# Pinning VectorE's reads of layer 0's fourth and fifth products between the sums of the output projection's left factors

## Chip, core and metric

The kernel runs on one core of a Trainium2 chip. The metric is the device time of one execution in microseconds (us), taken as the median of several runs. Five engines work side by side on the core. TensorE (PE in the profile, with its weight loads in a row of their own, PEld) does the matmuls and writes them to PSUM, the accumulation memory. VectorE (DVE) and ScalarE (ACT) read PSUM and work on SBUF, the on-chip memory. GpSimd (POOL) works on SBUF, and SyncE (SP) issues the transfers. Each engine runs its own instructions in the order in which the compiled program holds them, and waits on semaphores for the others.

## What is computed

64 graphs of 256 nodes with 512 features pass two layers that share one adjacency matrix. The reference, cut to what matters here:

```python
# layer 0: graph convolution, residual, layer norm
mi, mj = x @ Wi.T, x @ Wj.T
h = layernorm(x + deg[:, None] * (mi + b) + a @ mj)
# layer 1: masked attention of 8 heads of width 64, residual, layer norm
q, k, v = split_heads(h @ Wq.T + bq), ...(Wk, bk), ...(Wv, bv)
attn = softmax(where(adj == 0, -inf, q @ k.T / 8))
out = layernorm(h + merge_heads(attn @ v) @ Wo.T + bo)
```

Everything is float32.

## The kernel before

The 64 graphs are worked through in 32 groups of two. While the attention of one group runs, layer 0 of the next group runs between its steps. All large products use a seven-product scheme in place of the eight block products of a 2 x 2 block matrix multiplication. The left factors are the four blocks `A11`, `A12`, `A22` (and `A21`) and four sums of them, `S1` to `S4`. A product is eight matmuls (x 256 columns) and adds up in one PSUM bank. VectorE adds the bank to a tile in SBUF when a product is done; two of the banks are then accumulated into once more:

```python
def combine_left(f, order=anywhere):                       # L469
    nc.vector.tensor_add(f["S1"], f["A21"], f["A22"])      # L470
    nc.vector.tensor_sub(f["S2"], f["S1"], f["A11"])       # L471
    order(nc.vector.tensor_sub(f["S3"], f["A11"], f["A21"]))   # L472
    nc.vector.tensor_sub(f["S4"], f["A12"], f["S2"])       # L473

def l0_steps(b):                                           # layer 0, one graph
    ...
    def add_to(dst, src):
        nc.vector.tensor_add(dst, src, dst)                # L530
    ...
    def step4():
        product("y", "S2", T2, True)                       # fourth product
        add_to(place(0, 1), banks["y"])
    def step5():
        product("z", "S1", T1, True)                       # fifth product
        add_to(place(1, 1), banks["z"])
    def step6():
        product("y", "S3", T3, False)                      # adds to what is in bank y
        add_to(h, banks["y"]...)                           # both halves of a row block
        norm(xh[b][:, 1, :])
    def step7():
        product("z", "S4", B22, False)                     # adds to what is in bank z
        add_to(place(0, 1), banks["z"])
        norm(xh[b][:, 0, :])
```

So the seventh product may start only when VectorE has read what the fifth left in bank `z`, and the sixth only when it has read bank `y`.

`in_order` and `anywhere` say how the compile-time scheduler may place an instruction. `in_order` pins it behind the instruction that was written just before it for the same engine; `anywhere` leaves the scheduler free to place it by its own estimate of when it is ready. All matmuls are pinned, so TensorE follows the program text.

The place that the change is about comes once in each of the 31 turns of the main loop, after the last two pairs of heads of a group. `o` holds the steps of the output projection of group g (`o[0]` and `o[1]` use blocks of the attention's output that need no sums, later ones use `S1` to `S4` of `oS`, which `combine_left` makes). `rest` holds steps 4 to 7 of layer 0 for the second graph of group g + 1:

```python
inverses = divide_at_once(g, w + 1)   # twice: a reciprocal (L814), then a multiply into aoT (L815)
o = o_steps(g)
rest = work[SLOTS]
run(o[:1] + rest[:1] + o[1:2] + rest[1:2])
combine_left(oS[g], in_order)
end_values(inverses)                  # GpSimd: rtot += rden, twice (L820)
run(rest[2:] + o[2:5] + work[SLOTS + 1] + o[5:6] + work[SLOTS + 2] + o[6:])
```

`o[0]` ends in a ScalarE copy of its bank and two GpSimd additions to `xh` (L697 and L698, the second over 128 x 1024 elements). `o[1]` ends in a VectorE addition of its bank to `xh` (L691). The tile names in the profile are these: `po` is a bank of layer 0, `st` a bank of the projections, `xS` holds the left sums of layer 0, `oS` those of the output projection, and `aoT` is the attention's output. Every matmul has line L281, that of a helper.

Of the kernel before, what the change touches and what calls it, by code (L numbers as in the profile page):

```python
# [225 lines left out]
def unshifted_path(ctx, tc, flag, x, adj, wiT, wjT, b0, wqT, bq, wkT, bk, wvT, bv, woT, bo, out):  # L226
# [13 lines left out]
    nc = tc.nc  # L240
# [25 lines left out]
    def bank(name):  # L266
        return ps_m.tile([P, 512], F32, tag="mm", name=name)

    def score_banks(name):
        return ps_s.tile([P, 2, 512], F32, tag="sc", name=name)  # L270
# [9 lines left out]
    def matmul(*args, **kw):  # L280
        in_order(nc.tensor.matmul(*args, **kw))  # L281

    def transpose(*args):
        in_order(nc.tensor.transpose(*args))
# [6 lines left out]
    def load_x(b):  # L291
        if b < B:
            xh[b] = p6.tile([P, NT, D], F32, tag="xh", name="xh")
            nc.sync.dma_start(out=xh[b], in_=x[b].rearrange("(t p) d -> p t d", p=P))
# [67 lines left out]
    xhi, xlo, xl, xS, hT, hS, qT, kT, vv, aoT, oS = ({} for _ in range(11))  # L362
# [99 lines left out]
    def norm(t):  # L462
        norm_apply(t, *norm_stats(t))
# [2 lines left out]
        return {"A11": a11, "A12": a12, "A21": a21, "A22": a22,  # L466
                "S1": s[:, 0], "S2": s[:, 1], "S3": s[:, 2], "S4": s[:, 3]}

    def combine_left(f, order=anywhere):  # L469
        nc.vector.tensor_add(f["S1"], f["A21"], f["A22"])  # L470
        nc.vector.tensor_sub(f["S2"], f["S1"], f["A11"])  # L471
        order(nc.vector.tensor_sub(f["S3"], f["A11"], f["A21"]))  # L472
        nc.vector.tensor_sub(f["S4"], f["A12"], f["S2"])  # L473


    def input_tiles(b):
# [39 lines left out]
    def l0_steps(b):  # L516
        banks = {}

        def product(name, lname, n, first):
            if first:  # L520
                banks[name] = bank("po")[:, :H]
            for c in range(NC):
                matmul(banks[name], xS[b][lname][:, c, :], w0[:, n, c, :], start=(first and c == 0),
                                 stop=(c == NC - 1), skip_group_check=True)

        def place(t, j):
            return xh[b][:, t, j * H:(j + 1) * H]

        def add_to(dst, src):
            nc.vector.tensor_add(dst, src, dst)  # L530

        def step1():
            product("x", "A11", B11, True)
            u1 = p2.tile([P, H], F32, tag="lu", name="u1")
            nc.scalar.copy(u1, banks["x"])

            rest = xh[b].rearrange("p t (j o) -> p (t j) o", j=2)[:, 1:]
            nc.gpsimd.tensor_tensor(rest, rest, u1.unsqueeze(1).to_broadcast([P, 3, H]), ALU.add)  # L538

        def step2():  # L540
            product("w", "A22", T4, True)
            add_to(place(1, 0), banks["w"])

        def step3():
            product("x", "A12", B21, False)
            add_to(place(0, 0), banks["x"])

        def step4():
            product("y", "S2", T2, True)
            add_to(place(0, 1), banks["y"])  # L550

        def step5():
            product("z", "S1", T1, True)
            add_to(place(1, 1), banks["z"])

        def step6():
            product("y", "S3", T3, False)
            h = xh[b][:, 1, :].rearrange("p (j o) -> p j o", j=2)
            add_to(h, banks["y"].unsqueeze(1).to_broadcast([P, 2, H]))
            norm(xh[b][:, 1, :])  # L560

        def step7():
            product("z", "S4", B22, False)
            add_to(place(0, 1), banks["z"])
            norm(xh[b][:, 0, :])

        return [step1, step2, step3, step4, step5, step6, step7]

    def h_transpose(b, t, borrow=False):

        g, i = divmod(b, NB)
        if i == 0 and t == 1:
            hT[g] = p1.tile([P, NC, NB * N], F32, tag="hT", name="hT")
            hS[g] = pair_blocks(hT[g], "hS")
        pt = (score_banks("pt_h")[:, 0, :] if borrow else bank("pt_h")).rearrange("p (c n) -> p c n", c=NC)
        for c in range(NC):
            transpose(pt[:, c, :], xh[b][:, t, c * P:(c + 1) * P], ident)
        nc.scalar.copy(hT[g][:, :, i * N + t * P:i * N + (t + 1) * P], pt)
        if t == 0 and i == NB - 1:
            combine_left(hS[g])  # L580

    def add_output_bias(b):

# [3 lines left out]
    def pair_blocks(m, tag):  # L587

        s = p1.tile([P, 4, 2, N], F32, tag=tag, name=tag)
        return left_blocks(m[:, 0:2, 0:N], m[:, 2:4, 0:N], m[:, 0:2, N:2 * N], m[:, 2:4, N:2 * N], s)  # L590
# [186 lines left out]
    def values(g, w):  # L777
        i, pr = divmod(w, NC)
        if w == 0:
            aoT[g] = p1.tile([P, NC, NB * N], F32, tag="aoT", name="aoT")  # L780
            oS[g] = pair_blocks(aoT[g], "oS")
        pp = w % 2
        if pp == 0:
            pavs[g] = ps_v.tile([P, 2, N], F32, tag="av", name="pav")
        pe, _ = made[g, w]
        for kc in range(NT):
            for j in range(2):
                h0 = (2 * pr + j) * DH
                matmul(pavs[g][j * DH:(j + 1) * DH, pp, :], vv[g][:, i, kc, h0:h0 + DH], pe[:, j, kc, :],
                       start=(kc == 0), stop=(kc == NT - 1))  # L790

    def multiply():
        while products:
            d, spread = products.pop()
            in_order(nc.gpsimd.tensor_tensor(d, d, spread, ALU.mult))

    def divide_two(g, w):

        dst = target(g, w)
        nc.scalar.copy(dst, pavs[g])  # L800
        divide(dst, [made.pop((g, w - 1))[1], made.pop((g, w))[1]])

    def divide_at_once(g, w):


        den = bank("den").rearrange("p (r q) -> p r q", r=2)
        for pp in range(2):
            _, pk = made.pop((g, w - 1 + pp))
            for j in range(2):
                matmul(den[j * DH:(j + 1) * DH, pp, :], ones[:, :DH], pk[:, j, :], start=True, stop=True)  # L810
        inverses = []
        for pp in range(2):
            inverses.append(p2.tile([P, N], F32, tag="rden", name="rden"))
            in_order(nc.vector.reciprocal(inverses[pp], den[:, pp, :]))  # L814
            in_order(nc.vector.tensor_mul(target(g, w)[:, pp, :], pavs[g][:, pp, :], inverses[pp]))  # L815
        return inverses
# [29 lines left out]
    def layer0(g):  # L846

        b1, b2 = NB * g, NB * g + 1

        def item(f, *args):  # L850
            return lambda: f(*args)

        p, q = l0_steps(b1), l0_steps(b2)
        return [[item(l0_inputs, b1, 0, True), item(l0_inputs, b1, 1)],
                p[0:3] + [item(split_x, b2)] + p[3:4],
                p[4:7] + [item(l0_inputs, b2, 0)],
                [item(l0_inputs, b2, 1), q[0], q[1], item(h_transpose, b1, 1, True),
                 q[2], item(h_transpose, b1, 0, True)],
                q[3:],
                [item(h_transpose, b2, 1, True)], [item(h_transpose, b2, 0, True)]]  # L860

    def run(steps):
        for s in steps:
            s()
# [54 lines left out]
    for g in range(NG - 1):  # L919
        load_x(NB * (g + 2))  # L920
        load_x(NB * (g + 2) + 1)
        work = layer0(g + 1)
        run(work[0])
        for w in range(2, NB * NC, 2):
            values(g, w - 2)
            values(g, w - 1)
            multiply()
            divide_two(g, w - 1)
            later = [scores(g, w), scores(g, w + 1)]
            part = work[w // 2]  # L930
            n = 0 if w == NB * NC - 2 else 1
            run(later[:n] + part[:1] + later[n:] + part[1:])
        w = NB * NC - 2
        values(g, w)
        values(g, w + 1)
        multiply()
        inverses = divide_at_once(g, w + 1)
        o = o_steps(g)
        rest = work[SLOTS]
        run(o[:1] + rest[:1] + o[1:2] + rest[1:2])  # L940
        combine_left(oS[g], in_order)
        end_values(inverses)
        run(rest[2:] + o[2:5] + work[SLOTS + 1] + o[5:6] + work[SLOTS + 2] + o[6:])
        end = finish_steps(g)
        q = qk_steps(g + 1, qT, "qT", bq_sb, bqd)
        k = with_output_bias(g + 1, qk_steps(g + 1, kT, "kT", bk_sb, bkd))
        v = v_steps(g + 1)
        run(q[:5] + end[:1] + q[5:6] + end[1:2] + q[6:7] + end[2:3] + k[:1] + end[3:4] + k[1:] + end[4:] + v[:1])
        split_x(NB * (g + 2))
        run(v[1:5])  # L950
        run([scores(g + 1, 0), scores(g + 1, 1)])
        run(v[5:])
# [3 lines left out]
    g = NG - 1  # L956
# [89 lines left out]
```

## Time and profile before

| | before |
|---|---|
| median of 3 runs | 3230.88 us (3230.29 to 3233.19) |
| span of the profiled run | 3230.8 us |
| TensorE matmuls busy | 3189.2 us, 99% |
| TensorE weight loads busy | 2617.4 us, 81% |
| VectorE busy | 1892.0 us, 59% |
| GpSimd busy | 1506.9 us, 47% |
| ScalarE busy | 1113.0 us, 34% |
| granted TensorE clock | 0.998 |

The busy times are sums of instruction durations, so a stretch in which two matmuls overlap counts once and a gap not at all. One turn of the main loop takes about 99.7 us: the first and the last of the 31 instructions that make `S1` of `oS` start at 143.4 and 3134.1 us, and (3134.1 - 143.4) / 30 = 99.69.

In a timeline, the columns are the start and the duration in us, the engine, the line, the operation, what it writes and reads, the shape, and how many instructions of one kind were merged. In brackets stands the idle time of the engine before it and the instruction that ended this idle time. In a table of waits, the columns are the engine, tile and line that waited, the one it waited for, the total in us, how often, and the longest.

### The profile page before, as it was taken

The page shows a single profiled execution, that of the slowest core. Times are in us where ns is not written, and L with a number is a line of the kernel's source. Part 1 is how long each engine was busy: PE and PEld are TensorE (multiplying, and loading weights), DVE is VectorE, ACT ScalarE, POOL GpSimd, SP SyncE. Part 2 cuts the span into 40 slices and gives each one's busy share as a digit, 9 for nine tenths or more (in the row PEclk, how much of TensorE's full clock was granted, in tenths as well). Part 3 has the DMA queues.
Part 4 walks back from the last instruction along what each step waited for, and adds up shares of the span by engine and source line. Part 5 has one row for each costly group of instructions (what it writes and reads, how often), then busy time and mean ns, then how long its engine had stood idle before and what let it go on. Part 6 is the DMA issues. An engine that isn't in the chain of part 4 may idle for free. (4 is left out here: it accounts for less than half of the span.)

```text
span 3230.8 us, 48219 instructions
## 1 busy us (share of the span) xinstructions
PE 3189.2 (99%) x17398; PEld 2617.4 (81%) x17398; DVE 1892.0 (59%) x3847; ACT 1113.0 (34%) x2146; POOL 1506.9 (47%) x1191
## 2 busy tenths in 40 slices
PE   8999999999999999999999999999999999999998
PEld 6888888888888888888888888888888888888885
DVE  6655556555565555655556655556555565555665
ACT  2333333333333333333333333333333333333333
POOL 3454444544445444455444454344544445444443
PEclk9999999999999999999999999999999999999999
DMA  7234432344323433223443234432334322444223
GB/s 246 64 107 122 121 97 74 102 118 123 112 66 92 120 121 118 74 87 111 123 123 90 74 106 121 121 106 67 99 119 123 113 69 90 118 121 119 80 70 92
DMA packets 257168, 340.90 MB, mean 106 GB/s; under 512 B 29856, under 2 KB 154272, under 8 KB 256928
## 3 DMA queue, kind: packets, MB, share of 16 engines
q1 hardware_dynamic: 256928, 337.76, 34.9%
q8 instruction: 143, 2.34, 0.3%
q14 instruction: 97, 0.79, 0.1%
HBM read 274.73 MB, written 37.75 MB: 97 GB/s over the span
## 5 line engine op out<-in xcount | busy, mean ns | idle before, releaser
L454 POOL TENSOR_TENSOR rstd<-ve,mhalf 128x1 f32<-128x1 f32 x256 | 140.6, 549 | 813.6 <-DVE below L452 813.0
L281 PE MATMUL po<-w,xS 128*128 128x256 f32 x2048 | 474.9, 382 | 4.4 <-DVE xh L530 0.5
L281 PE MATMUL st<-hS,factor 128*128 128x256 f32 x2048 | 454.4, 380 | 2.5 <-DVE u L636 2.5
L763 POOL TENSOR_TENSOR pk<-pe 128x512 f32<-128x512 f32 x256 | 322.1, 1274 | 276.9 <-ACT pe L760 276.9
L281 PEld LDWEIGHTS po<-w,xS 128*128 128x128 f32 x2048 | 384.4, 190 | 77.4 <-DVE xh L530 17.2
L281 PEld LDWEIGHTS st<-hS,factor 128*128 128x128 f32 x2048 | 390.2, 191 | 56.3 <-DVE u L636 2.9
L281 PE MATMUL po<-w,xl 128*128 128x256 f32 x1536 | 360.1, 384 | 16.8 <-DVE xS L492 15.9
L760 ACT ACTIVATE pe<-pe 128x1024 f32<-128x1024 f32 x256 | 270.2, 1057 | 248.2 <-DVE pe L756 248.2
L281 PEld LDWEIGHTS po<-w,xl 128*128 128x128 f32 x1536 | 284.0, 190 | 73.3 <-PE po L281 22.9
L281 PE MATMUL st<-hT,factor 128*128 128x256 f32 x1536 | 342.2, 379 | 1.0 <-DVE qT L667 1.0
L636 DVE TENSOR_TENSOR u<-st,u 128x512 f32<-128x512 f32 x96 | 66.4, 692 | 468.8 <-PE st L281 461.6
L756 DVE TENSOR_TENSOR pe<-ps,maskT 128x1024 f32<-128x1024 f32 x256 | 297.1, 1201 | 67.6 <-PE ps L281 67.6
L530 DVE TENSOR_TENSOR xh<-po,xh 128x256 f32<-128x256 f32 (+1 forms) x384 | 170.5, 458 | 268.2 <-POOL xh L538 197.1
L281 PEld LDWEIGHTS st<-hT,factor 128*128 128x128 f32 x1536 | 291.7, 190 | 40.9 <-DVE qT L667 1.4
L281 PE MATMUL ps<-qT,kT 64*128 64x256 f32 x2048 | 256.5, 389 | 0.0
L281 PE MATMUL pav<-pe,v_sb 128*64 128x256 f32 x2048 | 250.1, 386 | 1.9 <-ACT pe L760 1.8
L281 PEld LDWEIGHTS ps<-qT,kT 64*128 64x128 f32 x2048 | 187.0, 186 | 68.2 <-issue 51.3
L281 PE MATMUL st<-factor,hS 128*128 128x256 f32 x1024 | 234.8, 382 | 0.0
L281 PE MATMUL st<-factor,oS 128*128 128x256 f32 x992 | 229.4, 379 | 0.0
L833 DVE RECIPROCAL rden<-den 128x256 f32<-128x256 f32 x96 | 168.8, 1758 | 91.6 <-PE den L281 86.1
L281 PEld LDWEIGHTS st<-factor,hS 128*128 128x128 f32 x1024 | 191.9, 190 | 35.4 <-issue 10.6
L459 ACT ACTIVATE shift<-below,rstd 128x1 f32<-128x1 f32 x256 | 75.4, 294 | 415.2 <-POOL rstd L454 409.6
(112 smaller groups left out, 5035.9 us busy)
## 6 DMA issues: line engine op xcount, KB each, us to landing
xh<-in_x_dram SPq DMA_DIRECT2D x64, 512.0 KB, 4.0
factor<-wq SPq DMA_DIRECT2D x128, 256.0 KB, 2.7
factor<-wk SPq DMA_DIRECT2D x128, 256.0 KB, 2.6
factor<-wv SPq DMA_DIRECT2D x128, 256.0 KB, 4.3
factor<-wo SPq DMA_DIRECT2D x124, 256.0 KB, 2.7
out_dram<-xh SPq DMA_DIRECT2D x62, 512.0 KB, 4.1
factor<-in_wqT_dram SPq DMA_DIRECT2D x96, 256.0 KB, 2.7
factor<-in_wkT_dram SPq DMA_DIRECT2D x96, 256.0 KB, 2.7
```

Of the source, the lines that this page charges most:

```text
L281: in_order(nc.tensor.matmul(*args, **kw))
L454: nc.gpsimd.tensor_tensor(rstd, ve, mhalf, ALU.pow)
L459: order(nc.scalar.activation(shift, below, AF.Identity, scale=rstd))
L530: nc.vector.tensor_add(dst, src, dst)
L636: nc.vector.tensor_add(new("u2"), bank["y"], k["u1"])
L756: nc.vector.tensor_add(pe.rearrange("p j t q -> p j (t q)"), ps.rearrange("p j t q -> p j (t q)"), maskT.rearrange("p t q -> p (t q)").uns ...
L760: in_order(nc.scalar.activation(flat, flat, AF.Exp, scale=QSCALE, accum_out=etot[:, NB * g + i, pr:pr + 1]))
L763: nc.gpsimd.tensor_tensor(pk, pe[:, :, 0, :], pe[:, :, 1, :], ALU.add)
L833: nc.vector.reciprocal(rden, den)
```

## The change

The four sums become a list of steps, so that other work can be written between them, and each of them can be pinned. At the end of the last two pairs of heads the first sum is moved ahead of layer 0's fifth product, and the other three follow it. The additions that read layer 0's fourth and fifth products are pinned as well. The aim is a fixed order on VectorE in which the bank of the fifth product is read right behind the first sum.

```diff
-    def combine_left(f, order=anywhere):
-        nc.vector.tensor_add(f["S1"], f["A21"], f["A22"])
-        nc.vector.tensor_sub(f["S2"], f["S1"], f["A11"])
-        order(nc.vector.tensor_sub(f["S3"], f["A11"], f["A21"]))
-        nc.vector.tensor_sub(f["S4"], f["A12"], f["S2"])
+    def left_steps(f, order=anywhere):
+        return [lambda: order(nc.vector.tensor_add(f["S1"], f["A21"], f["A22"])),
+                lambda: order(nc.vector.tensor_sub(f["S2"], f["S1"], f["A11"])),
+                lambda: order(nc.vector.tensor_sub(f["S3"], f["A11"], f["A21"])),
+                lambda: order(nc.vector.tensor_sub(f["S4"], f["A12"], f["S2"]))]
...
-        def add_to(dst, src):
-            nc.vector.tensor_add(dst, src, dst)
+        def add_to(dst, src, order=anywhere):
+            order(nc.vector.tensor_add(dst, src, dst))
...
         def step4():
             product("y", "S2", T2, True)
-            add_to(place(0, 1), banks["y"])
+            add_to(place(0, 1), banks["y"], in_order)
 
         def step5():
             product("z", "S1", T1, True)
-            add_to(place(1, 1), banks["z"])
+            add_to(place(1, 1), banks["z"], in_order)
...
         if t == 0 and i == NB - 1:
-            combine_left(hS[g])
+            for step in left_steps(hS[g]):
+                step()
...
-        run(o[:1] + rest[:1] + o[1:2] + rest[1:2])
-        combine_left(oS[g], in_order)
+        left = left_steps(oS[g], in_order)
+        run(o[:1] + rest[:1] + o[1:2] + left[:1] + rest[1:2] + left[1:])
         end_values(inverses)
```

No instruction is added or removed, and none changes its shape. The pins on steps 4 and 5 hold for all 64 graphs, not at this place alone. The sums of `hS`, the left factors of the query, key and value projections, stay free as they were.

## The prediction, made before the run

> **What bounds the kernel now.** I read the totals first, then the table of waits for TensorE, then the timeline of one turn of the main loop at the place that the diff touches.
>
> The totals give TensorE's matmuls 99% of the span, and no other engine more than 59%:
>
> ```profile
> PE 3189.2 (99%) x17398; PEld 2617.4 (81%) x17398; DVE 1892.0 (59%) x3847; ACT 1113.0 (34%) x2146; POOL 1506.9 (47%) x1191
> ```
>
> A change that only orders VectorE's instructions can therefore win no more than the time in which TensorE stands still: 3230.8 - 3189.2 = 41.6 us, 1.3% of the span. It could lose more than that. The table of waits says whether any of these 41.6 us belongs to the two reads that the diff pins. These are the rows of the weight loads, with total us, times and longest:
>
> ```profile
> PEld po L281 <- PE po L281: 22.9, 31, 1.1
> ...
> PEld po L281 <- DVE xh L530: 17.2, 32, 0.9
> ```
>
> The second row is the one. L530 is layer 0's addition that reads a bank, and `po` is that bank. It makes a weight load wait 32 times for 17.2 us in all; 31 of these are the turns of the main loop, 0.53 us each (31 x 0.53 = 16.4), and one of 0.9 us is in the start-up. The first row, also once a turn, belongs to an earlier product that waits for layer 0's inputs, and the diff doesn't touch it.
>
> The timeline of one turn in the middle of the run shows how the wait comes about:
>
> ```profile
> 1538.05 1.89 PE L281 MATMUL st<-factor,aoT 128*128 128x256 f32 x8
> ...
> 1538.42 2.36 POOL L698 TENSOR_TENSOR xh<-xh,u 128x1024 f32<-128x1024 f32 x1
> 1538.80 0.36 DVE L530 TENSOR_TENSOR xh<-po,xh 128x256 f32<-128x256 f32 x1
> 1539.08 0.41 DVE L815 TENSOR_TENSOR aoT<-pav,rden 128x256 f32<-128x256 f32 x1
> 1539.56 3.43 PEld L281 LDWEIGHTS po<-w,xS 128*128 128x128 f32 x16
> 1539.59 1.73 DVE L470 TENSOR_TENSOR oS<-aoT 128x512 f32<-128x512 f32 x1
> 1539.77 5.73 PE L281 MATMUL po<-w,xS 128*128 128x256 f32 x24
> ...
> 1540.72 1.19 POOL L820 TENSOR_TENSOR rtot<-rtot,rden 128x256 f32<-128x256 f32 x1
> 1541.24 0.68 DVE L691 TENSOR_TENSOR xh<-st,xh 128x512 f32<-128x512 f32 x1
> 1541.84 0.68 DVE L471 TENSOR_TENSOR oS<-oS,aoT 128x512 f32<-128x512 f32 x1
> 1542.44 0.68 DVE L472 TENSOR_TENSOR oS<-aoT 128x512 f32<-128x512 f32 x1
> 1543.04 0.41 DVE L530 TENSOR_TENSOR xh<-po,xh 128x256 f32<-128x256 f32 x1
> 1543.38 0.68 DVE L473 TENSOR_TENSOR oS<-aoT,oS 128x512 f32<-128x512 f32 x1
> 1543.51 1.59 PEld L281 LDWEIGHTS po<-w,xS 128*128 128x128 f32 x8 [0.53 <-DVE xh L530]
> ...
> 1545.34 1.89 PE L281 MATMUL st<-factor,aoT 128*128 128x256 f32 x8
> ```
>
> The 24 matmuls at 1539.77 are three products: layer 0's fifth (bank z), sixth (bank y) and seventh (bank z again). The seventh may not start before VectorE has read the fifth. That read is the L530 at 1543.04. The fifth product was done at about 1539.77 + 1.89 = 1541.66 (1.89 is what eight matmuls take in the first row), but VectorE then first made `S2` (L471) and `S3` (L472). The read ended at 1543.45, and the seventh product's weights went in at 1543.51, 0.53 us after they could have.
>
> What TensorE itself loses is less than 0.53, because the loads run ahead of the matmuls and catch up a little. From 1538.05 to 1539.77 one product takes 1.72 us, start to start. Three take 3 x 1.72 = 5.16; the trace has 1545.34 - 1539.77 = 5.57. **The loss is 0.41 us a turn**, or 12.7 us over 31 turns. A second reckoning: 24 matmuls of another layer 0 graph, at 1512.33 in the same turn, took 5.45 us, and 24 of the value projection at 1579.03 took 5.34, against 5.73 here; that is 0.28 to 0.39. I take 0.41, from the starts, as ends are modelled.
>
> **What the Trainium skill says.** Three places bear on this.
>
> - "TensorE: Matmul & The Clock Gate", Step-by-step: matmuls stay in program order, and only weight loads are pulled ahead. So TensorE can't fill the gap with the output projection's product behind it. The trace agrees: the product that follows starts at 1545.34, after all 24, though its inputs (`aoT`, the multiply L815) were complete at 1539.5 and the bank it writes had been read by 1541.9 (L691).
> - "SBUF — State Buffer", Who interferes with whom: a VectorE instruction with two SBUF inputs contends with a GpSimd instruction that reads SBUF, whoever starts first holds the port, and the other blocks fully; with at most one SBUF input it does not contend. The trace agrees. `S1` of `oS` (L470) takes 1.73 us here and 2.06 on average over 31, while the same sum for `hS` takes 0.68 on average over 32. Here it ends at 1541.32, 0.54 after the GpSimd addition L698 ended at 1540.78. The L691 and L530 additions, with one input in PSUM, keep their usual lengths.
> - "Perfetto Trace Analysis", Identifying the Most-Contended Engine: matmul occupancy is no good measure of headroom in TensorE. I use the 41.6 us only as a ceiling on what waits can cost; the gain itself comes from starts.
>
> **The change part by part.** No work is added or removed. What is written for VectorE in this stretch now is: second multiply (pinned), read of y (pinned), read of x (L691, free), `S1` (pinned), read of z (pinned), `S2`, `S3`, `S4` (pinned). A pin holds an instruction behind the one written before it, so this chain is fixed, except that the read of x might move up; its product ends too late for that. In the times of the turn above:
>
> 1. The second multiply follows the reciprocal directly, about 1538.9 to 1539.3, and the read of y comes behind it, 1539.25 to 1539.65. It was 0.45 earlier before. The sixth product loads its first weights at 1539.56 + 1.72 = 1541.28, so 1.6 us of slack remain.
> 2. The read of x is no longer behind `S1`. Its product ends at 1538.05 + 1.89 = 1539.94, so it runs at about 1540.0 to 1540.7. VectorE stands idle for some 0.4 us ahead of it. That costs nothing, for `S1` would have been blocked in this time.
> 3. `S1` is issued at about 1540.6 and is still held by L698 until 1540.78. It ends where it ended, at about 1541.33. The move of the read of x into the blocked time is what pays for everything after it.
> 4. The read of z waits for its product, 1541.66, and runs from 1541.7 to 1542.1. The weights of the seventh product want to load at 1543.51 - 0.53 = 1542.98. **The wait is gone, with 0.9 us to spare.**
> 5. `S2`, `S3`, `S4` follow at 0.60 us a step, and end at about 1543.9 instead of 1544.06. The first product that needs one of them comes in the load row behind 1545.13 + 1.73 = 1546.86 at the earliest: no new wait. The read of the sixth product follows at about 1543.85 (was 1543.98), and the norms behind it are no later than before. The transposes that need them start at 1550.5 in TensorE's row; the norm's last step for them ended at 1547.59. TensorE is 0.4 earlier now, and over 2 us of slack remain.
>
> Sum on TensorE's path: 31 x -0.41 = -12.7 us. Nothing is added to it. The pins at the other places change nothing that I can see: the trace already has the reads of y and z behind what is written before them (y behind two reads at 1506.43, z at 1514.42 behind the mask additions). Work that TensorE itself triggers moves up with it, so the gain should carry to the end. 3230.9 - 12.7 = 3218.2; I give back 0.3 for small changes in the schedule: **3218.5 us**, 0.4% less.
>
> **Rivals.**
>
> - *GpSimd takes the port first.* If L820 starts ahead of `S1`, `S1` waits another 0.73 us (the length of an unblocked L820), and ends near 1542.05; z is then read from 1542.0 to 1542.4, still 0.5 us in time. Against it: VectorE asks first. Time: the same 3218.
> - *The wait only changes its name.* `S1` written ahead of the read of z could hold it up when L698 runs late. It would have to be late by 0.9 us before TensorE waits again. L698 is triggered by TensorE's own product and in the trace lies within some tenths in every turn that I looked at (first, eighth, fifteenth, sixteenth, twenty-third, last). With half of the gain left: 3224 to 3225.
> - *The gain is given back later.* Some other chain of the turn, set by GpSimd or VectorE, could end last once TensorE is 0.4 earlier. For it: GpSimd and VectorE do run for long stretches without a gap. Against it: both have idle time that waits for TensorE in every turn, so they move with it. Time: 3226 to 3231.
> - *A pin hurts elsewhere.* The scheduler places by its own estimates; a read that it must now hold back, in any of the 64 graphs, could make TensorE wait. A tenth of a microsecond in each graph would cost 6 us. Time: 3225 to 3240.
>
> **Range and chances.** I give the full gain about 80%, and a little more or less of it comes from the two reckonings (0.28 to 0.41 a turn: 8.7 to 12.7 us). The other ways share the rest, mostly with part of the gain. The range is 3214.5 to 3226. A gain of 2% would need 65 us, more than all of TensorE's standing time, and a loss of 2% would need 2.1 us a turn; both are near zero.
>
> **What would show it.** Right: the row of weight loads that wait for L530 falls from 32 times and 17.2 us to about once and under 1 us. The 24 matmuls take about 5.3 us instead of 5.73. VectorE shows the order multiply, y, x, `S1`, z, `S2`, `S3`, `S4`, and `S1` takes about 0.7 to 0.8 instead of 2.06 on average, since it is issued late. A turn takes 99.28 us instead of 99.69. Wrong: a new waiter of TensorE at `po` or `st` with 31 entries, or an unchanged turn although this wait is gone. The prediction would fail if the scheduler moved something that I hold fixed.

## The result, and the profile after

The changed kernel takes 3219.63 us (median of 6 runs, 3216.64 to 3220.97), against 3231.64 us before (6 runs, 3230.29 to 3233.19). The ratio is 0.9961, with a 95% interval of 0.9949 to 0.9974: 12.0 us less. The prediction was 3218.5 us.

The totals of the changed kernel, on its page:

```profile
PE 3179.5 (99%) x17398; PEld 2625.4 (82%) x17398; DVE 1847.1 (57%) x3847; ACT 1108.6 (34%) x2146; POOL 1505.3 (47%) x1191
```

The number of instructions is the same on all engines. VectorE is busy for 44.9 us less than before (1892.0), though it does the same work; the reason is in `S1`, below. TensorE's stretches without work went from 41.6 to 3217.3 - 3179.5 = 37.8 us, 3.8 us less, though the time fell by 12.0. The rest was booked as busy. Each of the 24 matmuls below is recorded with a duration of 0.38 us, but they start 5.18 / 24 = 0.216 us apart. The record of one matmul therefore covers the first 0.16 us of a gap behind it, and the first matmul behind the gap is recorded as 0.48 us long. Of the 0.39 us that a turn lost before, only 0.12 us show as idle; over 31 turns these are the 3.8 us.

The weight loads' rows in the table of waits of the changed kernel:

```profile
PEld po L281 <- PE po L281: 23.2, 31, 1.1
...
PEld po L281 <- DVE xh L530: 0.9, 1, 0.9
```

The second row had 32 waits and 17.2 us. Only that of the start-up is left. The first row is as it was.

A turn of the changed kernel's main loop, in its timeline (the diff adds one line, so the former L691, L698, L815 and L820 are now L692, L699, L816 and L821):

```profile
1531.67 2.37 POOL L699 TENSOR_TENSOR xh<-xh,u 128x1024 f32<-128x1024 f32 x1
1531.82 0.42 DVE L816 TENSOR_TENSOR aoT<-pav,rden 128x256 f32<-128x256 f32 x1
1532.16 0.41 DVE L530 TENSOR_TENSOR xh<-po,xh 128x256 f32<-128x256 f32 x1
1532.81 5.16 PEld L281 LDWEIGHTS po<-w,xS 128*128 128x128 f32 x24
1533.03 5.34 PE L281 MATMUL po<-w,xS 128*128 128x256 f32 x24
...
1533.30 0.69 DVE L692 TENSOR_TENSOR xh<-st,xh 128x512 f32<-128x512 f32 x1 [0.72 <-PE st L281]
1533.90 0.68 DVE L470 TENSOR_TENSOR oS<-aoT 128x512 f32<-128x512 f32 x1
1533.98 1.19 POOL L821 TENSOR_TENSOR rtot<-rtot,rden 128x256 f32<-128x256 f32 x1
1534.95 0.42 DVE L530 TENSOR_TENSOR xh<-po,xh 128x256 f32<-128x256 f32 x1 [0.37 <-PE po L281]
1535.30 0.68 DVE L471 TENSOR_TENSOR oS<-oS,aoT 128x512 f32<-128x512 f32 x1
...
1538.21 1.89 PE L281 MATMUL st<-factor,aoT 128*128 128x256 f32 x8
```

The three products are one unbroken run of 24 matmuls. From their start to that of the next product it is 1538.21 - 1533.03 = 5.18 us, where it was 5.57. VectorE waits 0.37 us for the fifth product and reads it at once, from 1534.95 to 1535.37. `S1` (L470) takes 0.68 us; it had taken 1.73 in the turn shown before, 2.06 on average. A turn takes (3122.8 - 143.6) / 30 = 99.31 us by the starts of `S1`, 0.38 less than before, and 31 x 0.38 = 11.8 us.

### The profile page after: what moved, and what is told of

Same layout as the page of the kernel before. It is cut to its first block, busy times and chain, and to the rows that moved or that the text cites. A ratio compares the mean times of both kernels' runs of the same rounds, so it can differ in the third digit from the quotient of the medians.

```text
span 3217.3 us, 48188 instructions
## 1 busy us (share of the span) xinstructions
PE 3179.5 (99%) x17398; PEld 2625.4 (82%) x17398; DVE 1847.1 (57%) x3847; ACT 1108.6 (34%) x2146; POOL 1505.3 (47%) x1191
## 5 line engine op out<-in xcount | busy, mean ns | idle before, releaser
L281 PE MATMUL po<-w,xS 128*128 128x256 f32 x2048 | 467.2, 382 | 0.5 <-DVE xh L530 0.5
L761 ACT ACTIVATE pe<-pe 128x1024 f32<-128x1024 f32 x256 | 270.3, 1057 | 248.2 <-DVE pe L757 248.2
L281 PEld LDWEIGHTS po<-w,xl 128*128 128x128 f32 x1536 | 284.5, 191 | 72.2 <-PE po L281 23.2
L530 DVE TENSOR_TENSOR xh<-po,xh 128x256 f32<-128x256 f32 (+1 forms) x384 | 172.4, 463 | 279.7 <-POOL xh L538 197.0
L692 DVE TENSOR_TENSOR xh<-st,xh 128x512 f32<-128x512 f32 x186 | 144.9, 779 | 135.0 <-PE st L281 133.9
```

What stands on the lines that cost most here:

```text
L530: order(nc.vector.tensor_add(dst, src, dst))
L761: in_order(nc.scalar.activation(flat, flat, AF.Exp, scale=QSCALE, accum_out=etot[:, NB * g + i, pr:pr + 1]))
```

## The experiments

The change does four things to VectorE's order: the multiply comes ahead of the read of y, the read of x comes ahead of `S1`, the read of z comes ahead of `S2` and `S3`, and `S1` is out of GpSimd's way. My theory was that only one thing counts: the moment at which z is read. If that is later than the moment at which the seventh product's weights could load, TensorE loses time. Without a wait these weights go in 3.45 us after the first weights of the fifth product. The rivals: `S1` no longer held up by GpSimd is the gain; the pins in all 64 graphs are; or the read of x, moved into the blocked time, "is what pays for everything after it", as the prediction put it.

| kernel | VectorE's order | weights wait for z, a turn | time | ratio to before, 95% |
|---|---|---|---|---|
| before | y, mult, `S1`, x, `S2`, `S3`, z, `S4` | 0.53 us | 3231.6 | |
| changed | mult, y, x, `S1`, z, `S2`, `S3`, `S4` | none | 3219.6 | 0.9961 (0.9949 to 0.9974) |
| e1 | mult, y, x, z, `S1`, `S2`, `S3`, `S4` | none | 3219.9 | 0.9963 (0.9950 to 0.9977) |
| e2 | mult, y, x, `S1`, `S2`, `S3`, z, `S4` | 0.47 us | 3228.3 | 0.9993 (0.9985 to 1.0001) |
| e3 | mult, y, x, `S1`, `S2`, `S3`, `S4`, z | 1.07 us | 3249.7 | 1.0058 (1.0044 to 1.0072) |
| e4 | mult, y, `S1`, x, z, `S2`, `S3`, `S4` | none | 3220.2 | 0.9967 (0.9955 to 0.9979) |
| e5 | mult, y, `S1`, x, `S2`, `S3`, z, `S4` | 0.53 us | 3230.8 | 1.0002 (0.9993 to 1.0010) |
| e6 | y, mult, x, `S1`, z, `S2`, `S3`, `S4` | none | 3218.9 | 0.9967 (0.9955 to 0.9979) |
| e7 | as e2, GpSimd's `rtot` sums later | none | 3219.1 | 0.9964 (0.9950 to 0.9978) |
| e8 | as changed, and another place edited | none | 3236.4 | 1.0019 (1.0011 to 1.0026) |
| e9 | as changed, and that place mended | none | 3206.0 | 0.9922 (0.9909 to 0.9936) |

The waits are the row of L530 in each table of waits, less the 0.9 us of the start-up, over 31. Each ratio is to runs of the kernel before that were taken beside it (medians of 3230.5 to 3231.6 us). All edits are to the changed kernel.

**e1: z ahead of all sums.**

```diff
-        run(o[:1] + rest[:1] + o[1:2] + left[:1] + rest[1:2] + left[1:])
+        run(o[:1] + rest[:1] + o[1:2] + rest[1:2] + left)
```

> VectorE's order at the end of the last two pairs of heads becomes multiply, y, x, z, S1, S2, S3, S4: the read of the fifth product is ahead of all four sums. Theory (the read of z before its weights are wanted is all that counts): the read stands where it stood in the changed kernel, right behind its product, so the time is that of the changed kernel, 3219.6 us, within 2 us. The sums end 0.7 us later (S4 near 1537.9 in the times of the changed kernel's turn at 1533), and the norms behind them too, against some 2 us of slack. Rival (the place of S1 in the gap ahead of z is part of the gain): 31 x 0.7 us of it given back where the sums are late, 3225 to 3240 us.

Measured 3219.93 us. Whether `S1` comes ahead of the read or behind it makes no difference to the time. With `S1` behind it z is read no earlier, for the product isn't done earlier: VectorE only stands idle for 0.97 us ahead of the read instead of 0.37. The norms came later and cost nothing, but only just. The first norm's last step ends 0.12 us before its transposes load their weights, where the changed kernel has 1.75 us. I had expected the norms 0.7 us later; they came 1.7 us later.

**e2 and e3: z later and later.**

```diff
+        run(o[:1] + rest[:1] + o[1:2] + left[:3] + rest[1:2] + left[3:])   # e2
+        run(o[:1] + rest[:1] + o[1:2] + left + rest[1:2])                  # e3
```

> Order multiply, y, x, S1, S2, S3, z, S4: as before the change between S2 and S3, but with the read of x moved ahead of S1. Theory: z is read from about 1535.8 to 1536.2 in the times of the changed kernel's turn, and the seventh product's weights want to load at 1532.81 + 3.45 = 1536.26, so the read is just in time: 3219.6 to 3222 us. This would mean that moving x alone is worth nearly the whole gain. Rival (z must come right behind S1): some 3230 us, as before.

> Order multiply, y, x, S1, S2, S3, S4, z: S1 is out of GpSimd's way as in the changed kernel (0.68 us), but z is read behind all four sums, from about 1536.4 to 1536.8. Theory: the weights of the seventh product wait 0.6 us and TensorE loses 0.5 us a turn: 3219.6 + 31 x 0.5 = 3235 us (3231 to 3237), with the row of weight loads waiting for L530 back at 32 times and about 19 us. Rival (the gain came from S1 no longer being held by GpSimd's addition, 31 x 1.4 us of VectorE time): 3219 to 3221 us.

Both were slower than I expected: 3228.30 and 3249.72 us. e3 refutes the rival of the released `S1` all the same: there `S1` takes 0.68 us in every turn, and the kernel is 18.7 us slower than the runs of before beside it (3231.04). The timeline of e2 shows what I had left out:

```profile
1536.05 0.68 DVE L470 TENSOR_TENSOR oS<-aoT 128x512 f32<-128x512 f32 x1
1536.12 1.19 POOL L821 TENSOR_TENSOR rtot<-rtot,rden 128x256 f32<-128x256 f32 x1
1536.76 1.10 DVE L471 TENSOR_TENSOR oS<-oS,aoT 128x512 f32<-128x512 f32 x1
...
1538.39 0.41 DVE L530 TENSOR_TENSOR xh<-po,xh 128x256 f32<-128x256 f32 x1
...
1538.85 1.59 PEld L281 LDWEIGHTS po<-w,xS 128*128 128x128 f32 x8 [0.47 <-DVE xh L530]
```

`S1` had the port first and made GpSimd's L821 wait, then L821 had it and made `S2` (L471) wait: 1.10 us instead of 0.68. That is 0.42 us by which z is read later than I reckoned, and nearly all of the wait of 0.47. In the changed kernel VectorE's wait for the fifth product and the read of z, with one operand in PSUM, stand in just this place. e3 carries the same 0.42 and one sum more.

**e4: `S1` back in GpSimd's way, z where the change puts it.**

```diff
-        run(o[:1] + rest[:1] + o[1:2] + left[:1] + rest[1:2] + left[1:])
+        run(o[:1] + rest[:1] + left[:1] + o[1:2] + rest[1:2] + left[1:])   # and the read of x pinned
```

> Order multiply, y, S1, x, z, S2, S3, S4: S1 goes back into the time in which GpSimd holds it up, and the read of x comes behind it, both as before the change; z is still ahead of S2. Theory (only the moment of the read of z counts): S1 takes about 2.0 us and ends near 1534.6, x is read to 1535.2 and z from 1535.1 to 1535.5, 0.75 us ahead of the wish of the weights at 1536.26: 3219.6 us within 2 us. The prediction's step 2 held that the move of x into the blocked time is what pays; by that rival the gain shrinks, 3224 to 3231 us.

Measured 3220.16 us, inside the range of the changed kernel's runs. The timeline of e4 (the read of x is L705 here):

```profile
1528.99 2.35 POOL L699 TENSOR_TENSOR xh<-xh,u 128x1024 f32<-128x1024 f32 x1
...
1529.81 2.08 DVE L470 TENSOR_TENSOR oS<-aoT 128x512 f32<-128x512 f32 x1
...
1531.82 0.68 DVE L705 TENSOR_TENSOR xh<-st,xh 128x512 f32<-128x512 f32 x1
1532.42 0.41 DVE L530 TENSOR_TENSOR xh<-po,xh 128x256 f32<-128x256 f32 x1
```

`S1` takes 2.08 us again, x is read behind it, and still no weight load waits: z has been read by 1532.83, and the weights of that turn want to load at 1530.13 + 3.45 = 1533.58. VectorE is busy for 1882.8 us in e4 and for 1847.1 us in the changed kernel, and these 35.7 us bring nothing that the runs show. With z ahead of `S2` and `S3`, the move of x isn't needed either.

**e5 and e6: the two halves of the diff.** e5 keeps the pins on the reads and puts the sums back; e6 keeps the sums' places and frees the reads.

```diff
-        left = left_steps(oS[g], in_order)                                   # e5
-        run(o[:1] + rest[:1] + o[1:2] + left[:1] + rest[1:2] + left[1:])
+        run(o[:1] + rest[:1] + o[1:2] + rest[1:2])
+        combine_left(oS[g], in_order)                                        # as before
...
-            add_to(place(0, 1), banks["y"], in_order)                        # e6
+            add_to(place(0, 1), banks["y"])
-            add_to(place(1, 1), banks["z"], in_order)
+            add_to(place(1, 1), banks["z"])
```

> Only the reads of layer 0's fourth and fifth products are pinned; the four sums stand where they stood before. VectorE's order becomes multiply, y, S1, x, S2, S3, z, S4: the order before, but for the multiply and y, which change places. Theory (the moment of the read of z): z is still read behind S3, S1 is still held by GpSimd until its addition to xh ends, so nothing is won: 3229 to 3233 us, and 32 waits of about 17 us for L530's line. Rival (the pins in all 64 graphs bring the gain): 3219 to 3222 us.

> The other half: the sums are placed and pinned as in the changed kernel, and the reads of the fourth and fifth products are free. The scheduler then puts y ahead of the second multiply, and all else as in the changed kernel. Theory: the whole gain, 3219.6 us within 2 us. Rival (the pins on the reads are needed): 3224 us or more.

e5 took 3230.82 us, the time before. Its table of waits has the old row, under a new line number:

```profile
PEld po L281 <- DVE xh L536: 17.2, 32, 0.9
```

e6 took 3218.92 us, all of the gain. The pins on the reads neither help nor hurt; the sums' places in the text, with their pins, do it all (place and pin of the sums were not separated). The place of y ahead of the multiply or behind it is indifferent too.

**e7: e2 without GpSimd's sum behind `S1`.**

```diff
+        run(rest[2:])
         end_values(inverses)                      # both sums pinned behind the norms in rest[2:]
-        run(rest[2:] + o[2:5] + ...)
+        run(o[2:5] + ...)
```

> The order of e2 (z behind S3, x ahead of S1), but GpSimd's two sums of the reciprocals into rtot come behind layer 0's last norms. In e2 the second of them took the port behind S1 and held S2 up to 1.10 us instead of 0.68, and z was read 0.42 us later than I had reckoned. Theory: without it S2 takes 0.68 us, z is read in time or at most 0.1 us late, and the time is that of the changed kernel, 3219.6 to 3222 us. Rival (four instructions ahead of z are too many in any case): 3228 us, as e2.

Measured 3219.08 us. `S2` of this kernel follows `S1` and takes its plain length:

```profile
1533.61 0.68 DVE L470 TENSOR_TENSOR oS<-aoT 128x512 f32<-128x512 f32 x1
1534.32 0.69 DVE L471 TENSOR_TENSOR oS<-oS,aoT 128x512 f32<-128x512 f32 x1
...
1535.53 0.42 DVE L530 TENSOR_TENSOR xh<-po,xh 128x256 f32<-128x256 f32 x1
```

z is read until 1535.95; this turn's weights want it at 1532.51 + 3.45 = 1535.96. VectorE's order is the same as in e2, and the time is 9.2 us less for 0.4 us of port time a turn. Both of GpSimd's sums moved, but up to `S1` the turn is as in e2: in both `S1` starts 0.88 us after the fifth product. This explains e2's miss. It also shows a second way to the whole gain: z stays behind `S3`, and x moved into the blocked time is enough once L821 is out of the way.

**e8 and e9: the same question at another place.** In the slot ahead of this one, layer 0's left factors are summed (L489 to L492) behind two mask additions (`exponentials`, the scores plus `maskT`). A product waits there for the bank that the sums read. This is the row of 23.2 us above; it names a matmul as what ended the wait, but TensorE's own row in the changed kernel names the last of the sums:

```profile
PE po L281 <- DVE xS L492: 15.9, 32, 4.3
```

e8 writes the inputs between the two mask additions:

```diff
...
-            n = 0 if w == NB * NC - 2 else 1
-            run(later[:n] + part[:1] + later[n:] + part[1:])
+            if w == NB * NC - 2:
+                run(later[:1] + part[:1])          # part[0]: layer 0's inputs, second half
+                later[1](in_order)                 # mask addition pinned behind the sums
+                run(part[1:])
+            else:
+                run(later[:1] + part[:1] + later[1:] + part[1:])
```

> The changed kernel, and in the slot ahead of it the eight sums that make layer 0's left factors (L489 to L492) are placed between the two mask additions of 128 x 1024 elements instead of behind both. In the changed kernel a layer 0 product waits there for the last of these sums: 31 waits of its weight loads for 23.2 us (0.75 each), of which TensorE loses 0.37 us a turn (15.9 us less 4.3 in the start-up, over 31). Theory (the same kind of read, too late in VectorE's order): this wait goes, 31 x 0.37 = 11.5 us, 3208 us (3205 to 3213). Rival: the second mask addition, some 1.2 to 2 us later, makes its exponential and the matmuls that read it late, 3215 us or more.

Measured 3236.37 us: 16.7 us slower than the changed kernel. First the changed kernel's timeline, then that of e8:

```profile
1518.46 0.48 ACT L486 COPY xl<-pa 128x384 f32<-128x384 f32 x1 [0.23 <-PE pa L281]
1518.83 1.06 ACT L761 ACTIVATE pe<-pe 128x1024 f32<-128x1024 f32 x1
```

```profile
1526.25 1.06 ACT L761 ACTIVATE pe<-pe 128x1024 f32<-128x1024 f32 x1 [2.92 <-DVE pe L757]
...
1527.31 0.84 ACT L486 COPY xl<-pa 128x384 f32<-128x384 f32 x2
...
1527.82 0.73 PEld L281 LDWEIGHTS po<-w,xl 128*128 128x128 f32 x4 [0.83 <-ACT xl L486]
```

The edit also moved the pinned exponential (L761) ahead of ScalarE's copies of the same inputs (L486). TensorE now waited for a copy, and VectorE's sums, which read it, started late. This is not the rival that I had named. e9 splits mask addition and exponential, so that only VectorE's order changes:

```diff
...
+                e6, e7 = later
+                e6.mask()                          # VectorE
+                run(part[:1])                      # copies on ScalarE, sums on VectorE
+                e6.exponential()                   # ScalarE, behind the copies as before
+                e7.mask(in_order)
+                e7.exponential()
+                run(part[1:])
...
```

> e8 mended: in e8 the copies of layer 0's inputs (L486) had slipped behind the first exponential (1.06 us) on ScalarE, so the sums started later, not earlier: the first copy began 1.13 us after the first mask addition's end would have let it. Here the text keeps the copies ahead of both exponentials and only VectorE's order differs from the changed kernel: first mask addition, the eight sums, second mask addition. Theory: the first sum starts right behind the first mask addition, the last sum that the next product's bank waits for ends 0.7 us ahead of its wish, and the wait of 0.75 us at 31 weight loads goes, of which TensorE loses 0.37 us: 31 x 0.37 = 11.5 us, 3208 us (3206 to 3212). Rival: the later second mask addition and its exponential hold up GpSimd's sum of it and the matmuls that need that sum: 3214 us or more.

Measured 3205.95 us, ratio 0.9922 (0.9909 to 0.9936), faster than both kernels: 24.5 us less than the runs of before beside it (3230.49). The row of 23.2 us is gone from the table of waits. The timeline of e9:

```profile
1510.23 1.16 DVE L759 TENSOR_TENSOR pe<-ps,maskT 128x1024 f32<-128x1024 f32 x1
...
1511.36 3.17 PEld L281 LDWEIGHTS po<-w,xl 128*128 128x128 f32 x15
...
1511.54 0.29 DVE L489 TENSOR_TENSOR xS<-pa,xl 128x128 f32<-128x128 f32 x1
...
1513.51 1.21 DVE L759 TENSOR_TENSOR pe<-ps,maskT 128x1024 f32<-128x1024 f32 x1
```

The weight loads run on without a gap, and the second mask addition comes behind the sums. A turn takes (3110.7 - 144.5) / 30 = 98.87 us, 0.43 less than in the changed kernel. I had expected 0.37, and that this came so close is partly luck, for two errors nearly cancel. The place itself won more: from the product ahead of the wait to the transposes behind the product that waited, the matmuls take 1522.30 - 1518.26 = 4.04 us in the changed kernel and 1514.98 - 1511.53 = 3.45 us in e9, 0.59 less. I had reckoned with TensorE's idle time, which shows only a part of it. And the rival that I had named came true in part. GpSimd's sum (L768) of what the later mask addition feeds now comes late for the matmuls that read it:

```profile
PEld den L281 <- POOL pk L768: 8.6, 14, 1.8
```

In the turn shown above:

```profile
1517.91 1.28 POOL L768 TENSOR_TENSOR pk<-pe 128x512 f32<-128x512 f32 x1
...
1519.24 0.79 PEld L281 LDWEIGHTS den<-pk,ones 128*64 128x64 f32 x8
```

Here the weights load 0.05 us after the sum has ended; in the changed kernel 4.0 us lie between the two. From these matmuls to the output projection's first product a turn of e9 takes 0.17 us more than in the changed kernel, by the starts and on average over 31 turns. The margin that I had put at 0.7 us is smaller: the sum that frees the bank (an L492) ends at 1512.74, and the loads of the next product want it 1.65 us after the first, at 1513.01.

## Why the prediction was right, point by point

**The wait and its price: right.** 31 x 0.41 = 12.7 us was predicted; 12.0 us were measured, 0.38 us a turn by the trace. This lies at the upper end of the second reckoning (0.28 to 0.39). The first was a little high: three products without a wait take 5.18 us, not 5.16. What a late weight load costs TensorE follows from the series. In one turn each of e2, before and e3 the seventh product's weights wait 0.47, 0.53 and 1.07 us, and the three products take 5.52, 5.57 and 6.11 us from start to start. Against 5.18 that is a loss of 0.34, 0.39 and 0.93 us, so the loads catch up 0.13 to 0.14 us each time.

**The ceiling: wrong, without harm here.** The prediction held that no more can be won than TensorE's 41.6 us of standing time. But of the 13.5 us by which the profiled span fell, only 3.8 came out of that time, and 9.7 out of time booked as busy.

**Step 1, y behind the multiply: right, and free.** e6 has y ahead of it, and the same time.

**Step 2, the read of x "is what pays for everything after it": wrong.** e4 leaves x behind `S1` and has the full gain. What pays in the changed kernel is the read of z ahead of `S2` and `S3`, 1.2 us of sums at 0.60 a step. Moving x with z left behind `S3` (e2) brought about a quarter of the gain by the medians, (3231.0 - 3228.3) / 12.0; its interval runs from nothing to 4.8 us, 0.4 of the gain. Only with L821 out of the way as well (e7) is the move of x enough.

**Step 3, `S1` ends where it ended: right in the time, in part by coincidence.** It ended 0.54 us behind GpSimd's addition before, and 1534.58 - 1534.04 = 0.54 behind it after. But the prediction had it still held by that addition. It started 0.14 us ahead of the addition's end and took its plain 0.68 us: VectorE happened to be done with the read of x just as the port came free.

**Step 4, z in time with 0.9 us to spare: right.** z was read by 1535.37; the weights want to load at 1532.81 + 3.45 = 1536.26. But the reckoning missed why the place between `S1` and `S2` is a good one beyond being early: L821 takes the port behind `S1`, and `S2` in this place is held up by it (e2). A read with an operand in PSUM is not: the read of x (L692) takes 0.69 us inside the 2.37 us of GpSimd's L699.

**Step 5, no new wait: right, but the norms did come later.** `S4` ended 4.15 us after the fifth product's start; the prediction's times have 4.1. The norms were to be no later than before. The first one's last step ended 8.39 us after the fifth product's start, against 7.82 before, because the second read of z (1538.43) and the second norm's statistics (1538.87) now come ahead of the first norm's small steps on VectorE. Its slack ahead of the transposes went from 2.72 to 1.75 us, which was still enough. No row of TensorE or its loads grew by more than some tenths.

**The rivals.** Of GpSimd taking the port first, the wait changing its name, a gain given back later and a pin that hurts elsewhere, none came. e5 shows the last one directly: the pins alone change nothing.

## What to carry to other kernels

Look in the bound engine's table of waits for reads that free a bank or an operand, and place each such read by the moment at which it is wanted: ahead of anything the same engine could do later, but not earlier than needed. Slacks of 0.75 us and 0.01 us brought the same time here (e4, e7), and with all sums behind the read (e1) VectorE waited idle for the product, and the norms were left with only 0.12 us of slack. Sums that other engines want only microseconds later go behind it. When moving one engine's instruction, compare the order of all engines: e8 lost 16.7 us against the changed kernel through a copy that slipped behind an exponential on a third engine, and e9 won 13.7 us with the same aim. Idle time in TensorE's row was no measure of what such a wait costs here: of 0.39 us lost, 0.12 us were idle. The distance from start to start showed all of it.

## What the hardware showed that I had not expected

A wait for the port that VectorE and GpSimd share does not show as idle time. It lies inside the recorded duration: 2.06 us for a sum that takes 0.68, and the 44.9 us by which VectorE's busy time fell without any work removed are mostly 31 x (2.06 - 0.68) = 42.8 us of it. The blocked sums of 0.68 us end 0.54 to 0.55 us after the recorded end of the GpSimd instruction in the three kernels shown that have one (before, e2, e4). In the changed kernel a sum that starts 0.14 us ahead of that end is not lengthened. So the port seems to come free some 0.14 us ahead of the recorded end. This is read from these ends alone; no run measured it by itself.
